# Attention and expert routing on one core: values with the routing, sort in steps, outputs held back, transposes in pairs

## Chip, core and metric

The kernel runs on one core of a Trainium2 chip. The metric is the device time of one execution in microseconds. The kernel before was run three times: 777.58 us in the median, 776.79 to 778.72.

## What is computed

The reference takes x of 4 batches of 1024 tokens of 256 channels, all in float32, and returns `x + attention(xn) + ffn(xn)` with `xn = layernorm(x)`.

```python
xn = layernorm(x)
# attention, 16 heads of 16 channels
q, k, v = heads(xn @ w_q.T), heads(xn @ w_k.T), heads(xn @ w_v.T)
sq = elu(q) + 1
coarse = (sq @ M) / clip(sq @ z)                 # M, z: the four memories summed
fine = sum(softmax(mean over tokens of n_f) * (sq @ memory_m) / clip(n_f))
p = sigmoid(relu(coarse @ eg_w1.T + eg_b1) @ eg_w2.T + eg_b2)
memory = p * fine + (1 - p) * coarse
local = causal_linear_attention(q, k, v, chunk=128)
attention = (g * memory + (1 - g) * local) @ w_o.T    # g = sigmoid(memory_gate)
# ffn: 8 experts of 176, two for each token, and a shared one of 352
cw = normalized top-2 of softmax(xn @ gate_weight.T)
ffn = sum_e cw[e] * swiglu_e(xn) + swiglu_shared(xn)
```

## The kernel before

The 4096 tokens are 8 blocks of 512 (`NBLK`, `TB`), each of 4 tiles of 128 (`NT`); there are 32 tiles (`NTT`). The instructions of each engine run in the order in which the program issues them, and that order is written by hand: a unit is a function with a weight, `mix` merges several streams of units by their share of the total weight, `split` cuts one stream into equal parts, and `run` issues a list. There is no planner beside it.

- **Routing** (`statistics`, `normalize`, `transpose_x`, `logits`). x is loaded on SP's queue, six blocks ahead (`AHEAD`); the weights come on ACT's queue. Each block is normalized in place, written to `xns` in DRAM (later gathered by row), transposed into `xnT`, and multiplied with the gate weights. The reciprocal square root is taken on POOL for two blocks at a time. The first queries are among these units.
- **Sort** (`route`, `sort`, `slots`, `shift_logits`, `weights`, `owners`). DVE finds the two experts of each token and gives each pair a slot; the slots of an expert fill whole tiles, 71 at most (`NST`). `invert` then builds one-hot matrices, three tiles at a time, POOL scales them (`held`, L510), and `add_slots` multiplies them into one PSUM bank (`found`) that lists which token and weight each slot has. These units are mixed with keys and values of block 0, the shared expert of block 0 and the first two attention rounds.
- **Attention rounds.** Round n does, for tile n: `scores` into four PSUM banks (`quad`), `mask` on DVE, `keys_back` (a transpose of the keys), `memory` into the same banks, `weigh` and `fine` on DVE and POOL, `local`, `back` and `update` of the running state. For tile n-1 it does the gate: `turned` transposes coarse, `gate_hidden` multiplies it with `w1` (L830) and ACT takes the relu, `gate_out` multiplies with `w2` (the `pz` matmul, L840). For tile n-2 `turned` transposes o and `output` multiplies the shared expert's hidden layer and o (L895, L899) into `po`.
- **Beside them**, in four parts for each block: `project` for keys and queries, `values` (L578), `shared_gate` and `shared_up`.
- **Experts**, spread over rounds 2 to 29 (`first_round`, `last_round`). For each of 71 slot tiles: `fetch` gathers 128 rows of `xns` on POOL's queue and loads the expert's weights on SP's, `expert_in` transposes the rows (`pxg`, L959), `expert_hidden` multiplies with gate and up (`phe`, L968), `expert_turn` transposes the result (`pTe`, L982), `expert_out` multiplies with down (`pye`, L991), and `put` adds the rows into `sums` in DRAM with an indirect DMA on POOL (L1000). `sums` starts as a copy of x.
- **Tail.** Once all puts have landed, `totals` reads `sums` for tiles 0 to 27, adds the kept outputs on POOL and writes the result; tiles 28 to 31 load their part with `residual` and are added where `output` evicts them.

TensorE's results go through a ring of four PSUM banks (`bank`), shared by everything but `quad`.

Of the kernel before, what the change touches and what calls it, by code (L numbers as in the profile page):

```python
# [8 lines left out]
FP = mybir.dt.float32  # L9
# [5 lines left out]
P = 128  # L15
NT = 4
# [6 lines left out]
def linear_attention_moe_kernel(  # L23
# [51 lines left out]
    AHEAD = 6  # L75
# [10 lines left out]
    big = ctx.enter_context(tc.tile_pool(name="big", bufs=AHEAD))  # L86
# [3 lines left out]
    ps_q = ctx.enter_context(tc.tile_pool(name="ps_q", bufs=1, space=bass.MemoryType.PSUM))  # L90
# [6 lines left out]

    quad = ps_q.tile([P, NG, 512], FP, tag="quad", name="quad")

# [4 lines left out]
    def load_x(blk):  # L104
        xb = big.tile([P, NT, H], FP, tag="tok", name=f"x_{blk}", bufs=AHEAD)
        nc.sync.dma_start(
            xb, x[blk * TB : (blk + 1) * TB, :].rearrange("(n p) h -> p n h", p=P)
        )
        st["x", blk] = xb

    for blk in range(AHEAD):
        load_x(blk)

    def load_weight(w, name):
        t = const.tile([P, NC, w.shape[1]], FP, tag=name, name=name)
        nc.scalar.dma_start(t, w.rearrange("(k p) c -> p k c", p=P))
        return t

    wvg = load_weight(w_vg, "wvg")
    wq = load_weight(w_q, "wq")  # L120
    wk = load_weight(w_k, "wk")
    raw = const.tile([P, NC, NMN, D1], FP, tag="raw", name="raw")
    nc.scalar.dma_start(
# [3 lines left out]
    nc.scalar.dma_start(gate, memory_gate.to_broadcast([P, NH]))  # L127
    b2 = const.tile([P, 1], FP, tag="b2", name="b2")
    nc.scalar.dma_start(b2, eg_b2.to_broadcast([P, 1]))
    w1 = load_weight(eg_w1, "w1")  # L130
    b1 = const.tile([HID, 1], FP, tag="b1", name="b1")
    nc.scalar.dma_start(b1, eg_b1)
    w2 = const.tile([HID, 1], FP, tag="w2", name="w2")
    nc.scalar.dma_start(w2, eg_w2)
# [5 lines left out]
    nc.scalar.dma_start(  # L140
# [3 lines left out]
    if full < NF:  # L144
        nc.scalar.dma_start(wd[: FS - full * P, full, :], w_down[FR + full * P :, :])
# [12 lines left out]
    neghalf = const.tile([P, 2, NT], FP, tag="neghalf", name="neghalf")  # L158
# [64 lines left out]
    alive = const.tile([P, NMN], FP, tag="alive", name="alive")  # L223
    ungate = const.tile([P, NH], FP, tag="ungate", name="ungate")
# [26 lines left out]
    def memories_by_group():  # L251
# [3 lines left out]
        for m in range(3, NMN):  # L255
            nc.vector.tensor_add(raw[:, :, 0, :], raw[:, :, 0, :], raw[:, :, m, :])
        for c in range(NC):
# [18 lines left out]
    def living():  # L276

        norms = small.tile([P, NC, NMN], FP, tag="norms", name="norms", bufs=1)
        nc.vector.tensor_copy(norms, raw[:, :, :, HD])
# [8 lines left out]
    def statistics(blk):  # L288

        xb = st["x", blk]  # L290
        if blk % 2 == 0:
            st["mv"] = small.tile([P, 2, NT, 2], FP, tag="mv", name=f"mv_{blk}", bufs=3)
            st["rstd"] = small.tile([P, 2, NT], FP, tag="rstd", name=f"rstd_{blk}", bufs=3)
        mv, rstd = st["mv"], st["rstd"]
        for i in range(NT):
            stats = small.tile([P, 6], FP, tag="stats", name=f"stats_{blk}_{i}")
            nc.vector.bn_stats(stats, xb[:, i, :])
            nc.vector.bn_aggr(mv[:, blk % 2, i, :], stats)
        if blk % 2:
            nc.vector.tensor_scalar(rstd, mv[:, :, :, 1], LN_EPS, None, ALU.add)  # L300
            nc.gpsimd.tensor_tensor(rstd, rstd, neghalf, ALU.pow)
        st["norm", blk] = mv[:, blk % 2], rstd[:, blk % 2]

    def normalize(blk):
# [9 lines left out]
        nc.vector.tensor_scalar(  # L314
            xb[:, NT - 1, :], xb[:, NT - 1, :], mv[:, NT - 1, 0:1], rstd[:, NT - 1 : NT],
            ALU.subtract, ALU.mult,
        )
        for i in range(NT - 1):
# [7 lines left out]
        if blk + AHEAD < NBLK:  # L326
            load_x(blk + AHEAD)

# [13 lines left out]
    def logits(blk):  # L342

        xnT = st["xnT", blk]
        pl = bank(f"pl_{blk}").rearrange("p (i e) -> p i e", i=NT)
        for i in range(NT):
            for k in range(NC):
                nc.tensor.matmul(
                    pl[:, i, :], xnT[:, k, i * P : (i + 1) * P], wvg[:, k, H + E - P : H + E],
                    start=(k == 0), stop=(k == NC - 1),  # L350
                )
        nc.scalar.copy(lgs[:, blk * NT : (blk + 1) * NT, :], pl[:, :, P - E :])

    def route(half):
# [12 lines left out]
        def first_largest(v, best, m, name):  # L367

            nc.vector.tensor_tensor(m, v, spread(best), ALU.is_equal)
            nc.vector.tensor_mul(m, m, first[:, None, :].to_broadcast(sh))  # L370
            at = t2(name + "_at")
            nc.vector.tensor_reduce(at, m, AX.X, ALU.max)
            nc.vector.tensor_tensor(m, m, spread(at), ALU.is_equal)

# [3 lines left out]
        first_largest(lg, best, m1, "m1")  # L378
# [4 lines left out]
        first_largest(rest, low, m2, "m2")  # L383
        st["best", half] = best

    def shift_logits():
# [8 lines left out]
        nc.scalar.activation(gatew, gatew, AF.Exp)  # L395

    def weights():
# [4 lines left out]
        nc.vector.reciprocal(tot, tot)  # L402
        nc.vector.tensor_mul(gatew, gatew, tot[:, :, None].to_broadcast(sh))
        two = st["two"]
        both = tmp.tile([P, 2, NTT, E], FP, tag="h", name="chosen", bufs=2 * NF)
        nc.vector.tensor_mul(both, picks, gatew[:, None].to_broadcast([P, 2, NTT, E]))
        nc.vector.tensor_reduce(two, both.rearrange("p r i e -> p (r i) e"), AX.X, ALU.add)
        nc.vector.tensor_add(tot, two[:, :NTT], two[:, NTT:])
# [3 lines left out]
        nc.vector.tensor_mul(t2, t2, tot[:, None, :].to_broadcast([P, 2, NTT]))  # L412

    def sort():
# [5 lines left out]
        nc.vector.tensor_add(both, pick[0], pick[1])  # L420
        pp = bank("pp").rearrange("p (w i e) -> p w i e", w=2, e=E)
# [5 lines left out]
        st["pp"] = pp  # L427

    def slots():
        work, pp = st.pop("work"), st.pop("pp")  # L430

        cnt = work[:, 1].rearrange("p (e i) u -> p e (i u)", e=E)
        nc.vector.tensor_copy(cnt, pp[:, 0].rearrange("p i e -> p e i"))
        upto = work[:, 2].rearrange("p (e i) u -> p e (i u)", e=E)
# [306 lines left out]
    def update(n):  # L741

        if n % (BPB * NT) == last_of_batch:
            return
# [464 lines left out]
```

## Time and profile before

| | |
|---|---|
| median of three runs | 777.58 us |
| the profiled execution: time, span | 782.79 us, 781.1 us |
| TensorE busy, mean granted clock | 700.7 us (90%), 0.956 |
| DVE, POOL, ACT busy | 426.1, 400.3, 273.8 us |
| bytes moved | 81.48 MB, mean 104 GB/s |

The profile is of one execution, with times from the start of its span. In names such as `phe L968` the number is a line of the kernel. A matmul in float32 appears as two records, a transpose as one. A matmul's busy time includes the drain of its pipeline, so records next to each other overlap. In the stage tables the columns are: the stretch, its length, the busy time of TensorE, of its weight loads (PEld), of DVE, ACT and POOL, each with the number of instructions, then the granted TensorE clock, the busy share of the DMA engines and GB/s. In the lists of groups, `busy, mean ns | idle before` is followed by what ended the idle time.

### The profile page before, as it was taken

What the parts mean: (1) busy time and instruction counts of PE and PEld (TensorE: products, weight loads), DVE (VectorE), ACT (ScalarE), POOL (GpSimd) and SP (SyncE); (2) the same over time, 40 slices, a digit from 0 to 9 for tenths busy, and PEclk for the clock granted to TensorE, in tenths of its full rate; (3) what the DMA queues carried; (4) which work ended last, traced back from release to release, by engine and by line L of the source; (5) the groups of instructions that cost most, each with busy time, mean ns of one, the idle gap of its engine ahead of it and who ended that gap; (6) DMA issues with size and microseconds to landing.
All of it is one profiled execution on the core that took longest, in us unless ns stands there. A gap on an engine that the chain in (4) does not pass through costs nothing.

```text
span 781.1 us, 14630 instructions
## 1 busy us (share of the span) xinstructions
PE 700.7 (90%) x5268; PEld 491.0 (63%) x5268; DVE 426.1 (55%) x1084; ACT 273.8 (35%) x707; POOL 400.3 (51%) x441
## 2 busy tenths in 40 slices
PE   1798579499999999999999999999999999999965
PEld 0675356366676666666667667666766667767653
DVE  6536857445446744455536644554457555655553
ACT  2563002123443333433443343433443344334300
POOL 3100366506555656464546555556545646657576
PEclk9899689889999999999999999999999999999976
DMA  9554000234343453344444443443443444454285
GB/s 283 183 178 134 1 0 1 59 107 97 84 117 85 90 118 84 86 106 94 97 111 92 103 104 84 93 113 84 97 104 85 107 101 103 108 123 99 29 261 171
DMA packets 86373, 81.48 MB, mean 104 GB/s; under 512 B 7437, under 2 KB 83901, under 8 KB 86173
## 3 DMA queue, kind: packets, MB, share of 16 engines
q1 hardware_dynamic: 69661, 59.64, 26.5%
q0 software_dynamic: 13632, 18.62, 14.3%
q10 hardware_dynamic: 3008, 2.28, 0.9%
q8 instruction: 42, 0.69, 0.4%
q14 instruction: 30, 0.25, 0.1%
HBM read 62.56 MB, written 22.15 MB: 108 GB/s over the span
## 4 chain that ended last, share of the span: by engine, by line
PE 76%; DVE 7%; DMA 5%; POOL 4%; ACT 3%; issue 3%; SPq 0%; POOLq 0%; DVEq 0%; ACTq 0%
PE phe L968 12%; PE pye L991 8%; PE po L895 5%; PE psu L871 5%; PE pg L856 5%; PE quad L658 4%; PE pn L684 4%; PE po L899 3%; PE pv L578 3%; PE pq L550 3%; PE pk L550 3%; PE quad L770 3%; PE pxg L959 2%; PE pTe L982 2%; PE ph L830 2%
## 5 line engine op out<-in xcount | busy, mean ns | idle before, releaser
L1000 POOL DMA_INDIRECT sums<-y,islot x71 | 112.7, 1588 | 81.0 <-DMA sums<-y,islot 29.9
L792 POOL TENSOR_TENSOR cg<-coarse,gates 128x256 f32<-128x256 f32 x32 | 23.7, 742 | 165.1 <-DVE coarse L785 164.9
L968 PE MATMUL phe<-wgu,xgT 128*128 128x352 f32 x284 | 100.9, 478 | 1.1 <-ACT hTe L984 0.9
L665 DVE TENSOR_TENSOR sT<-quad,causal 128x512 f32<-128x512 f32 x128 | 80.2, 682 | 14.3 <-PE pk L736 6.5
L933 POOL DMA_INDIRECT xg<-xns,islot x71 | 71.3, 1005 | 15.9 <-issue 8.8
L991 PE MATMUL pye<-wdn,hTe 88*128 88x256 f32 x284 | 76.6, 392 | 1.8 <-ACT oT L822 1.0
L968 PEld LDWEIGHTS phe<-wgu,xgT 128*128 128x128 f32 x284 | 49.9, 191 | 25.3 <-issue 5.3
L810 POOL TENSOR_TENSOR fm<-fm 128x512 f32<-128x512 f32 x32 | 43.6, 1363 | 36.5 <-DVE prob L843 23.1
L974 DVE SCALAR_TENSOR_TENSOR the<-the,phe 128x176 f32<-128x176 f32 x71 | 23.8, 335 | 69.6 <-ACT the L973 66.8
L991 PEld LDWEIGHTS pye<-wdn,hTe 88*128 88x128 f32 x284 | 49.5, 189 | 15.1 <-issue 5.5
L995 ACT ACTIVATE y<-pye,wslot 128x256 f32<-128x256 f32 x71 | 33.6, 473 | 58.6 <-PE pye L991 55.7
L895 PE MATMUL po<-wd,h 128*128 128x256 f32 (+1 forms) x192 | 49.2, 394 | 0.0
L973 ACT ACTIVATE the<-phe 128x176 f32<-128x176 f32 x71 | 22.5, 318 | 74.5 <-PE phe L968 72.5
L871 PE MATMUL psu<-xnT,wu 128*128 128x512 f32 (+1 forms) x96 | 47.6, 620 | 0.0
L856 PE MATMUL pg<-xnT,wg 128*128 128x512 f32 (+1 forms) x96 | 47.0, 613 | 0.7 <-ACT nT L691 0.7
L799 DVE TENSOR_TENSOR fm<-quad,rw 128x512 f32<-128x512 f32 x64 | 42.0, 682 | 0.0
L863 DVE SCALAR_TENSOR_TENSOR th<-th,pg 128x512 f32<-128x512 f32 (+1 forms) x24 | 16.4, 684 | 43.8 <-ACT th L862 39.6
L876 DVE SCALAR_TENSOR_TENSOR h<-th,psu 128x512 f32<-128x512 f32 (+1 forms) x24 | 16.5, 686 | 42.9 <-PE psu L871 42.2
L961 ACT COPY xgT<-pxg 128x256 f32<-128x256 f32 x71 | 26.5, 373 | 37.1 <-PE pxg L959 18.3
L895 PEld LDWEIGHTS po<-wd,h 128*128 128x128 f32 (+1 forms) x192 | 36.1, 200 | 4.3
L558 DVE SCALAR_TENSOR_TENSOR sqT<-pq,eq 128x512 f32<-128x512 f32 x16 | 11.1, 692 | 50.8 <-ACT eq L556 50.7
L563 DVE SCALAR_TENSOR_TENSOR skT<-pk,ek 128x512 f32<-128x512 f32 x16 | 11.1, 691 | 49.8 <-ACT ek L556 47.1
(195 smaller groups left out, 1510.2 us busy)
## 6 DMA issues: line engine op xcount, KB each, us to landing
wgu<-in_w_gate_dram SPq DMA_DIRECT2D x71, 176.0 KB
wgu<-in_w_up_dram SPq DMA_DIRECT2D x71, 176.0 KB
wdn<-in_w_down_dram SPq DMA_DIRECT2D x71, 176.0 KB
x<-in_x_dram SPq DMA_DIRECT2D x8, 512.0 KB
xns<-x SPq DMA_DIRECT2D x8, 512.0 KB
sums<-in_x_dram SPq DMA_DIRECT2D x8, 512.0 KB
part<-sums SPq DMA_DIRECT2D x14, 256.0 KB
out_dram<-acc SPq DMA_DIRECT2D x14, 256.0 KB
```

Of the source, the lines that this page charges most:

```text
L550: nc.tensor.matmul(pq, w[:, k, c * P : (c + 1) * P], xnT[:, k, :], start=(k == 0), stop=(k == NC - 1),)
L665: nc.vector.tensor_mul(sT, quad[:, g, :].rearrange("p (c t) -> p c t", t=P), causal[:, None, :].to_broadcast([P, NC * 2, P]),)
L799: nc.vector.tensor_mul(fm[:, c].rearrange("p g m (r k) -> p g (m r) k", k=HD), quad[:, :, c * KM + KX + KN : (c + 1) * KM].rearrange("p g ...
L810: nc.gpsimd.tensor_add(fm[:, :, 0:2, :], fm[:, :, 0:2, :], fm[:, :, 2:4, :])
L856: nc.tensor.matmul(pg[:n, :], wg[:, k, f * P : f * P + n], xnT[:, k, :], start=(k == 0), stop=(k == NC - 1),)
L871: nc.tensor.matmul(pu[:n, :], wu[:, k, f * P : f * P + n], xnT[:, k, :], start=(k == 0), stop=(k == NC - 1),)
L895: nc.tensor.matmul(po[:, :H], st["h", blk, f][:k, tok], wd[:k, f, :], start=(f == 0), stop=False)
L933: nc.gpsimd.indirect_dma_start(out=xg, out_offset=None, in_=xns, in_offset=bass.IndirectOffsetOnAxis(ap=islot[:, j : j + 1], axis=0),)
L968: nc.tensor.matmul(ph[:, : 2 * F], xgT[:, k, :], wgu[:, k].rearrange("p g f -> p (g f)"), start=(k == 0), stop=(k == NC - 1),)
L991: nc.tensor.matmul(py[:, :H], hT[:, f, :], wdn[:, f, :], start=(f == 0), stop=(f == 1))
L995: nc.scalar.activation(y, py[:, :H], AF.Copy, scale=wslot[:, j : j + 1])
L1000: nc.gpsimd.indirect_dma_start(out=sums, out_offset=bass.IndirectOffsetOnAxis(ap=islot[:, j : j + 1], axis=0), in_=st.pop(("y", j)), in_of ...
```

## The change

The kernel after does the same arithmetic with these edits:

- **Loads.** All eight blocks of x are loaded at the start on SP's queue. Only the weights of values, queries and keys stay on ACT's queue; the others follow x on SP's.
- **Values with the routing.** `values` works on two tiles, with the gate weights as eight more columns, and gives the logits as well; the separate `logits` go. The values of all blocks are computed in the routing and are written into the tile that held x. The routing's order is a written list. Queries move out of it.
- **Statistics.** Block 0 takes its reciprocal square root alone, the others in pairs 1-2, 3-4, 5-6, and 7 alone. DVE normalizes two of four tiles, not one.
- **Sort in steps.** `route`, `sort`, `slots` (now in `sort`), `weights` and `owners` are generators, cut into 32 steps that are mixed with the queries of blocks 0 to 2, keys of 0 and 1 and the shared expert of block 0. `projected` and `shared_hidden` hold the last DVE step of a projection and are issued one unit later.
- **Lists in rounds 0 to 3.** `invert`, `hold` and `add_slots` stand three batches apart; ACT scales the tokens, POOL the weights. The experts run over rounds 4 to 29, after a pause of weight 2000.
- **Gate.** coarse becomes the stationary operand and `w1` the moving one; bias, relu, the product with `w2` and its sum are on DVE, and `pz` goes.
- **Transposes.** `turned` takes o of tile n-2 and coarse of n-1 in one bank with one copy; `keys_back` takes two tiles every second round; `expert_turn` takes the hidden layer of slot tile j and the gathered rows of j+2 in one bank with one copy.
- **Outputs held back.** The outputs of tiles 24 to 31 are computed after round 29, mixed with rounds 30 and 31, and add their part of `sums` on DVE; `totals` covers tiles 0 to 23. Results are written on ACT's queue.
- Some buffers shrink (`nT`, `loc`, `coarse`, `cg`, `o`, `sk` to one, `xg` from four to three).

```diff
-    for blk in range(AHEAD):
+    for blk in range(NBLK):
         load_x(blk)
...
-    def logits(blk):
+    def values(blk, pair):
+        xnT, wide = st["xnT", blk], st["wide", blk]
+        if pair == 0:
+            st["va", blk] = wide[:, :, : NH * D1].rearrange("p i (h k) -> p i h k", k=D1)
+        va = st["va", blk]
+        pv = ps_v.tile([P, 2, 512], FP, tag="v", name=f"pv_{blk}_{pair}")
+        for j in range(2):
+            i = 2 * pair + j
             for k in range(NC):
                 nc.tensor.matmul(
-                    pl[:, i, :], xnT[:, k, i * P : (i + 1) * P], wvg[:, k, H + E - P : H + E],
+                    pv[:, j, : H + E], xnT[:, k, i * P : (i + 1) * P], wvg[:, k, :],
                     start=(k == 0), stop=(k == NC - 1),
                 )
...
+        nc.scalar.copy(
+            va[:, tiles, :, :HD], pv[:, :, :H].rearrange("p i (h k) -> p i h k", k=HD)
+        )
+        nc.scalar.copy(lgs[:, first : first + 2, :], pv[:, :, H : H + E])
...
+    def hold(lo):
...
+        for k in range(n):
+            nc.scalar.activation(
+                held[:, k, 0], tiles[:, k], AF.Copy, scale=token[:, lo + k : lo + k + 1]
+            )
+        nc.gpsimd.tensor_mul(
+            held[:, :, 1], tiles, st["two"][:, lo : lo + n, None].to_broadcast([P, n, NST])
+        )
...
+    def turned(n):
+        srcs = [(s, m) for s, m in (("o", n), ("coarse", n + 1)) if 0 <= m < NTT]
+        pt = bank(f"pt2_{n}").rearrange("p (s c t) -> p s c t", s=2, t=P)
...
     def gate_hidden(n):
...
-                ph[:HID, :P], w1[:, c, :], cT[:, c, :], start=(c == 0), stop=(c == NC - 1)
+                ph[:, :HID], cT[:, c, :], w1[:, c, :], start=(c == 0), stop=(c == NC - 1)
-        nc.scalar.activation(h1, ph[:HID, :P], AF.Relu, bias=b1)
+        nc.vector.tensor_add(h1, ph[:, :HID], b1)
+        nc.vector.scalar_tensor_tensor(h1, h1, 0.0, w2, ALU.max, ALU.mult, accum_out=z)
...
     def gate_out(n):
...
-        nc.tensor.matmul(pz[:, :1], st.pop(("h1", n)), w2, start=True, stop=True)
-        nc.scalar.activation(prob, pz[:, :1], AF.Tanh, bias=b2, scale=0.5)
+        nc.scalar.activation(prob, st.pop(("z", n)), AF.Tanh, bias=b2, scale=0.5)
...
+    def expert_turn(j):
+        fetch_rows(j + 4)
+        fetch_weights(j + 3)
+        pt = bank(f"pte_{j}").rearrange("p (f t) -> p f t", t=P)
+        lo, hi = (0 if j >= 0 else 2), (4 if j + 2 < NST else 2)
+        if j >= 0:
+            for f in range(2):
+                nc.tensor.transpose(pt[:, f, :], hidden[j % 2][:, f * FH : f * FH + P], ident)
+        if j + 2 < NST:
+            xg = st.pop(("xg", j + 2))
+            for c in range(NC):
+                nc.tensor.transpose(pt[:, 2 + c, :], xg[:, c * P : (c + 1) * P], ident)
+        dst = exp.tile([P, 4, P], FP, tag="turned", name=f"turned_{j}")
+        nc.scalar.copy(dst[:, lo:hi], pt[:, lo:hi])
...
-    first_round, last_round = 2, 30
+    first_round, last_round = 4, 30
...
+    ahead = "S0 S1 masks N0 T0 S2 S3 N1 N2 V0 T1 T2 S4 memories V1 S5 N3 N4 V2 T3 T4 S6 gates V3 S7"
+    ahead += " N5 N6 V4 living T5 T6 N7 V5 route V6 T7 V7"
...
+    first_pairs = queries(0) + queries(1) + keys(0) + shared(0) + keys(1) + queries(2)
+    start = [u for u in late(first_pairs) if u]
...
+    run(mix(steps(sorting(), 32, 1000), start))
...
+    for k, lo in enumerate(batches):
+        lists += [(400, invert, lo)]
+        lists += [(100, hold, batches[k - 1])] if k else []
+        lists += [(768, add_slots, batches[k - 2])] if k > 1 else []
...
+    units = [(10, residual, n) for n in range(held_from, held_from + 3)]
+    outs = {n: [(1280, output, n, True)] for n in range(held_from, NTT)}
...
+    units[2:2] = [(1800, lambda: None)]
+    tail = mix([u for n in range(last_round, NTT) for u in rounds[n]], units)
```

In the written list S is `statistics`, N `normalize`, T `transpose_x` and V `values` of a block; `held_from` is 24.

## The prediction

> **What bounds the kernel now.** I read the page first, then a table of busy time by stage, the start times of TensorE's instructions in the middle, and the chain that ended last. From the page: TensorE's share, the granted clock in 40 slices, and the dearest group on POOL.
>
> ```profile
> PE 700.7 (90%) x5268; PEld 491.0 (63%) x5268; DVE 426.1 (55%) x1084; ACT 273.8 (35%) x707; POOL 400.3 (51%) x441
> ...
> PEclk9899689889999999999999999999999999999976
> ...
> L1000 POOL DMA_INDIRECT sums<-y,islot x71 | 112.7, 1588 | 81.0 <-DMA sums<-y,islot 29.9
> ```
>
> Five of the first nine slices show 6 or 8 tenths of the clock, the last two 7 and 6: TensorE starves in the first quarter and at the end. The stages, cut at 70 (routing), 146 (sort, lists, rounds 0 and 1), 156 (first gathered rows land), 733 (rounds 2 to 29 with the experts) and 742 (last put lands):
>
> ```profile
> 0.00:70.00 70.00, 45.78 (x238) 35.34 (x239) 35.38 (x151) 30.87 (x66) 10.99 (x35) 0.93 0.68 217
> 70.00:90.00 20.00, 12.88 (x73) 6.52 (x71) 17.26 (x50) 2.98 (x7) 0.52 (x1) 0.81 0.00 0
> 90.00:120.00 30.00, 22.86 (x147) 17.45 (x148) 16.28 (x31) 1.90 (x4) 20.08 (x28) 0.77 0.00 1
> 120.00:146.00 26.00, 23.38 (x170) 17.66 (x168) 21.70 (x46) 6.94 (x16) 18.11 (x29) 1.00 0.00 1
> 146.00:156.00 10.00, 0.58 (x4) 0.29 (x2) 2.83 (x7) 1.38 (x3) 4.62 (x5) 0.66 0.37 105
> 156.00:733.00 577.00, 565.08 (x4390) 389.74 (x4388) 312.92 (x758) 223.13 (x596) 314.04 (x315) 0.99 0.43 98
> 733.00:742.00 9.00, 7.21 (x103) 5.61 (x102) 3.05 (x6) 2.96 (x9) 5.06 (x5) 1.00 0.28 32
> 742.00:781.00 39.00, 22.91 (x152) 18.36 (x152) 16.69 (x37) 3.60 (x10) 26.86 (x26) 0.69 0.67 216
> ```
>
> The columns after the length are TensorE, its weight loads, DVE, ACT, POOL, clock, DMA share and GB/s. The middle is TensorE at 98%; from 70 to 156 TensorE has 59.7 us of work in 86, behind DVE and POOL; the tail moves 8.4 MB of sums and outputs in 39 us.
>
> Busy time counts a group's pipeline tail, so I price TensorE work from start to start:
>
> ```profile
> 410.14 0.38 PE L840 MATMUL pz<-w,h 64*128 64x1 f32 x2
> 410.45 0.44 PE L959 MATMUL pxg<-ident,xg 128*128 128x128 f32 x2
> 410.73 0.60 PE L700 MATMUL pb<-ident,nT 128*128 128x128 f32 x4
> ```
>
> pz is shown as 0.38 but costs 0.31, and the two transposes 0.28. The chain of waits over 156 to 733, summed by line, gives such prices for all lines. An attention round costs 8.4 us (scores 1.15, memory 0.79, local 1.02, back 1.03, update 0.47, output 2.16, gate_hidden 0.58, pz 0.31, transposes of o, coarse and keys 0.27, 0.34, 0.28). An expert step costs 2.82 (phe 1.30, pye 0.96, pxg 0.29, pTe 0.27). A block's keys and queries cost 3.5 each, shared projections 10.8, values 3.6. Check: 28 rounds, 71 steps and 6.5 blocks without the last queries give 235 + 200 + 136 = 571 of the measured 577.
>
> **The change, stage by stage.** The sum is made for the profiled execution: span 781.1, time 782.79, so 1.7 around it; the median of the runs is 777.58, a factor of 0.9933.
>
> *Front, to the end of the last values: 67 us.* Block 0 gets its own rstd, so transposes start near 12 instead of 16. All logits matmuls go (eight groups of 16 at 1.79 us, 14.3), 8 columns are added to each value matmul, and all values come in (8 x 3.7). Values write into x's own tile, so ACT's first copy waits until the write of xns from that tile has landed, and behind it on ACT are the copies of blocks 1 and 2, for which TensorE waits. On SP's queue lie 4.2 MB of x, 1.4 of weights now moved there and the 0.5 written; with 0.8 on ACT's queue that is 7 MB. The first 20 us moved 286 GB/s, so it lands near 25 to 28, and TensorE, with transposes of blocks 0 to 2 and values 0 done (4 + 3.7, cold at first), idles from about 22 to 29. What such a gap does to the clock is shown by the same stretch of before:
>
> ```profile
> 25.00:30.00 5.00, 2.46 (x19) 1.79 (x17) 2.46 (x10) 1.78 (x4) 0.00 (x0) 0.97 0.43 138
> 30.00:35.00 5.00, 3.78 (x20) 3.59 (x20) 2.69 (x13) 1.15 (x4) 0.25 (x1) 0.68 0.87 301
> 35.00:40.00 5.00, 4.09 (x19) 3.62 (x20) 2.34 (x19) 4.74 (x11) 1.70 (x3) 0.66 0.36 126
> ```
>
> Two half-idle slices cost about 3 us at a clock of 0.67. The Trainium skill (TensorE: Matmul & The Clock Gate, Part 1) speaks against a change that opens such a gap: after an idle window of about 3.4 us the clock halves, until a window of that length is busy. By it the cost is an estimated 1.7 us; I keep the row's 3.
>
> From 29 on there are 7 x 3.7 of values and 5 x 1.33 of transposes, 33 us, and 5 for the cold clock and the last block's copies: 67. ACT (3.7 per block: two normalizations of 0.53, four copies) and DVE (3.3) stay under TensorE's 5.2. Ends 60 (the write lands early) and 76 (every xns takes 5.9 us to land, as the second did).
>
> *Sort: 35 us.* 16 projection units of 1.76 to 1.79, 28.4, and 1.5 of small matmuls; beside them DVE has about 14 of sort steps, 6 of projected and 8 of gating, 4 of batch weights: 32. The two are nearly equal and DVE serves in order, so 35; ends 31 and 42.
>
> *Rounds 0 to 3 with the lists: 72 us.* TensorE: four rounds without pz, two of them without output, shared(1), 128 found matmuls of 0.13: 53. DVE: 8.7 per round less 2 (33), shared gating 8.2, invert 22 times. An invert costs 0.92 (L499 0.37, L503 0.55) where POOL rests and 1.6 (0.71, 0.89) beside L510; half of L510 moves to ACT, so I take 1.15: 25. DVE sums to 66 and now sets the pace; with waits for scores and memory 72, ends 63 and 84. The first rows' landing (4.25) lies under the pause ahead of the experts.
>
> *Rounds 4 to 29: 502 us.* Per round pz goes (0.31), and o and coarse stand side by side, and where pairs already did, they started 0.21 to 0.22 apart instead of 0.27 and 0.34: 0.18. So 7.9 x 26 = 205. gate_hidden moves 64 columns instead of 128 but loads 128 instead of 64; I book no gain, since even pz with one moving column takes 0.15 each. Outputs 24 to 27 leave (8.6). Experts 71 x 2.77 = 197, by the same reason. Gathers move behind put and out on POOL and stay two turns ahead of use; weights stay three ahead on SP. Projections of blocks 2 to 7: 6 x 17.8 less 3.5, 103, and 1.5 for batch weights. Sum 498, and 1% as in before. The added DVE pair in gate_hidden (some 0.45) replaces 0.36 on ACT and pz's wait; DVE, at 11.2 per round now (312.92 over 28), hides it. ACT loses a fixed part of one copy per expert step (0.373 + 0.363 against 0.59 for 512 columns) and is no bound. Buffers cut to one are read and rewritten a round apart. Ends 486 (turns gain 0.15 more each) and 525 (a round of 20.2).
>
> *Tail: 44 us against 48 from 733.* The last put still lands some 8 after the last experts. Eight outputs (17) stand where TensorE was idle 18 us, and loads no longer queue behind outputs on SP. But ACT, which issues the outputs now, waits for POOL's totals, and behind it are nT and the turned copies of rounds 30 and 31. The chain shows that the DMA sets this pace:
>
> ```profile
> 738.21 3.71 DMA sums<-y,islot
> ...
> 743.41 4.40 DMA part<-sums
> ```
>
> The same 8.4 MB at 237 GB/s (740 to 760) takes 35, plus the end of the chain. Ends 38 and 52.
>
> Sum 67 + 35 + 72 + 502 + 44 = 720, with 1.7 it is 721.7, times 0.9933: 717.
>
> **Rivals.** *The middle is held by something else than TensorE's issue.* Its weight loads are busy 389.7 of 577 and some 40 us of the chain there are ACT, DVE and issue. Then a round keeps its 20.6, 26 x 20.6 = 536, and the time is 751. Against it: the priced instructions fill 571 of 577. The Trainium skill (Perfetto Trace Analysis, Identifying the Most-Contended Engine) says matmul busy time is a poor measure of headroom and the share of weight loads a better one; by it (68% here) TensorE would not be the limit, which is this case. Chance 0.17.
>
> *Front, lists and tail at their good ends* (60, 31, 63, 502, 38): 691 to 700; DVE would have to run the lists without waits. 0.12.
>
> *Slower: POOL's puts.* A put waits on POOL for the one before it to land, and gathers and attention's sums stand behind it. POOL's work per round becomes 5.3 for attention, 2.73 x 1.59 puts and 2.73 x 1.0 gathers, 12.4. If each put took the cycle of the last two (3.71 to land and 1.57 before, 5.3), a round would need 5.3 + 2.7 + 14.4 = 22.4 us: 582 for the middle, 797 in all. It turns slower from 21.7 per round. For it: steps come every 7.0 us instead of 8.1, and each merged turn now holds the hidden layer until the gathered rows are there. Against: waits for earlier puts total 29.9 us over 71, and 7.0 is above 5.3. 0.09, and 0.03 for a balance within 0.3%, about what a measurement of this kernel tells from no change.
>
> **Numbers.** The forecast, 717 (700 to 738), has 0.59. The ends of the terms, taken together as independent, give some 25 either way; the first rival reaches 751. So 694 to 750. Faster 0.88, same 0.03, slower 0.09.
>
> **What would show it.** Values end near 67 and the first scores start near 102. TensorE is near 98% busy from 174 to 676, a round taking 19.3. In rounds 0 to 3 DVE is over 85% busy. If TensorE is near 98% and rounds still take 20.6, my prices are wrong; if TensorE is idle there behind pte or phe, POOL's puts are the place to look. A front past 76 means that the copies of values wait for xns.

## The result, and the profile after

The changed kernel takes 731.43 us in the median of four runs (731.18 to 731.93); the kernel before, run beside it, takes 778.15. The ratio is 0.9397, with a 95% interval of 0.9373 to 0.9422: 6% faster. The forecast was 717, its range 694 to 750. The profiled execution took 731.18 us with a span of 729.5. From here on "the changed kernel" is this one, and experiments are compared by their ratios to the kernel before, since chips differ by a few tenths of a per cent.

The page of the changed kernel, with the rows that answer to those of before:

```profile
PE 653.1 (90%) x5084; PEld 465.3 (64%) x5084; DVE 455.9 (62%) x1193; ACT 266.8 (37%) x614; POOL 386.0 (53%) x436
...
PEclk9799989999999999999999999999999999999598
...
L1058 POOL DMA_INDIRECT sums<-y,islot x71 | 113.4, 1597 | 70.6 <-DMA sums<-y,islot 15.1
```

TensorE has 47.6 us less work and keeps its 90%. Of the first nine slices of the clock two are below 9 (a 7 and an 8) instead of five; near the end there is a 5. Waits of a put for the put before it fell from 29.9 to 15.1 us, although the experts now run in two rounds fewer: the slower rival, POOL's puts, found nothing to stand on.

The stages, cut where the last values end, where the scores of rounds 0, 4 and 30 start, and at the end of the last put:

```profile
0.00:60.30 60.30, 40.98 (x197) 34.76 (x198) 29.49 (x133) 27.27 (x64) 13.41 (x68) 0.92 0.69 222
60.30:89.50 29.20, 29.00 (x73) 12.92 (x71) 23.82 (x66) 14.00 (x25) 0.00 (x0) 1.00 0.19 64
89.50:165.10 75.60, 58.88 (x573) 45.56 (x573) 63.10 (x142) 27.99 (x89) 35.43 (x45) 0.93 0.06 15
165.10:672.00 506.90, 489.54 (x3957) 344.50 (x3956) 315.68 (x795) 191.89 (x422) 306.82 (x293) 0.99 0.49 111
672.00:682.80 10.80, 3.36 (x57) 2.53 (x56) 5.70 (x15) 0.53 (x2) 6.20 (x7) 0.75 0.27 33
682.80:729.50 46.70, 31.39 (x234) 24.99 (x234) 18.11 (x45) 5.15 (x14) 24.09 (x24) 0.83 0.57 180
```

Against the forecast's terms: front 60.3 (67), sort 29.2 (35), rounds 0 to 3 75.6 (72), rounds 4 to 29 506.9 (502), tail 57.5 (44). The differences are -6.7, -5.8, +3.6, +4.9 and +13.5, in all +9.5. Against before, cut at the same scores: round 4 starts at 165.1 instead of 201.3, rounds 4 to 29 take 506.9 instead of 531.7, and from round 30 to the end it is 57.5 instead of 48.1; that is -36.2 - 24.8 + 9.4 = -51.6, the whole difference of the spans. So the tail gives back 9.4 of 61.0 us, and that is where the forecast is furthest off.

The forecast of 717 is 14.4 us below the measured 731.43. The terms account for 9.5 of that. The other 5 come from the factor 0.9933: the profiled execution of before was slower than its kernel's median, that of the changed kernel was not (731.18 against 731.43). And 9.5 is a small remainder of large misses: -12.5 in the front and the sort against +13.5 in the tail. That they nearly cancel is luck.

What TensorE waited for, by line (total, times, longest), of the changed kernel:

```profile
PE ph L879 <- ACT oc L868: 14.4, 2, 12.0
PE pt L344 <- ACT x L331: 11.2, 1, 11.2
PE found L568 <- POOL held L560: 9.6, 6, 3.0
PE quad L806 <- DVE sT L698: 9.1, 5, 2.4
PE pv L362 <- ACT xnT L347: 8.2, 2, 7.8
```

The second is the start. Of the others, three name places to test: the tail behind ACT (first), the lists behind POOL's `held` (third), the front behind ACT's copies of the transposed xn (last).

### The profile page after: what moved, and what is told of

It is laid out like the page before. It is cut to its first block, busy times and chain, and to the rows that moved or that the text cites. A ratio compares the mean times of both kernels' runs of the same rounds, so it can differ in the third digit from the quotient of the medians.

```text
span 729.5 us, 14268 instructions
## 1 busy us (share of the span) xinstructions
PE 653.1 (90%) x5084; PEld 465.3 (64%) x5084; DVE 455.9 (62%) x1193; ACT 266.8 (37%) x614; POOL 386.0 (53%) x436
## 5 line engine op out<-in xcount | busy, mean ns | idle before, releaser
L1058 POOL DMA_INDIRECT sums<-y,islot x71 | 113.4, 1597 | 70.6 <-DMA sums<-y,islot 15.1
L1042 DVE SCALAR_TENSOR_TENSOR hidden<-hidden,phe 128x176 f32<-128x176 f32 x71 | 23.8, 335 | 122.4 <-ACT hidden L1041 122.4
L1036 PE MATMUL phe<-wgu,turned 128*128 128x352 f32 x276 | 96.9, 474 | 2.5 <-ACT turned L1029 2.1
L1049 PE MATMUL pye<-wdn,turned 88*128 88x256 f32 x284 | 75.5, 388 | 4.2 <-PE pu L786 3.0
L1036 PEld LDWEIGHTS phe<-wgu,turned 128*128 128x128 f32 x276 | 48.5, 191 | 26.2 <-issue 6.4
L1049 PEld LDWEIGHTS pye<-wdn,turned 88*128 88x128 f32 x284 | 50.1, 189 | 20.1 <-issue 8.5
L846 POOL TENSOR_TENSOR fm<-fm 128x512 f32<-128x512 f32 x32 | 41.7, 1304 | 26.2 <-DVE prob L892 13.1
L1041 ACT ACTIVATE hidden<-phe 128x176 f32<-128x176 f32 x71 | 22.6, 318 | 86.7 <-PE phe L1036 79.7
L1029 ACT COPY turned<-pte 128x512 f32<-128x512 f32 (+1 forms) x71 | 41.2, 580 | 35.6 <-PE pte L1027 34.6
L362 PE MATMUL pv<-wvg,xnT 128*128 128x264 f32 x128 | 33.1, 420 | 8.2 <-ACT xnT L347 8.2
L806 PE MATMUL quad<-mem,sqT 32*128 32x170 f32 x512 | 27.6, 328 | 9.1 <-DVE sT L698 9.1
L894 DVE SCALAR_TENSOR_TENSOR o<-diff,prob,loc 128x256 f32<-128x256 f32 x32 | 33.1, 1035 | 3.4
```

The costliest lines, as they stand in the source:

```text
L846: nc.gpsimd.tensor_add(fm[:, :, 0:2, :], fm[:, :, 0:2, :], fm[:, :, 2:4, :])
L1029: nc.scalar.copy(dst[:, lo:hi], pt[:, lo:hi])
L1036: nc.tensor.matmul(ph[:, : 2 * F], xgT[:, k, :], wgu[:, k].rearrange("p g f -> p (g f)"), start=(k == 0), stop=(k == NC - 1),)
L1049: nc.tensor.matmul(py[:, :H], hT[:FH, f, :], wdn[:, f, :], start=(f == 0), stop=(f == 1))
L1058: nc.gpsimd.indirect_dma_start(out=sums, out_offset=bass.IndirectOffsetOnAxis(ap=islot[:, j : j + 1], axis=0), in_=st.pop(("y", j)), in_of ...
```

## The experiments

### The tail: who issues the outputs

In the tail of the changed kernel, ACT's waits and its timeline read so:

```profile
ACT oT L865 <- POOL acc L980: 22.5, 2, 15.8
ACT oT L865 <- DMA out_dram<-acc: 6.7, 1, 6.7
```
```profile
687.86 0.46 ACTq L981 DMA_DIRECT2D out_dram<-acc  x1
688.36 0.37 ACT L865 COPY oT<-pt 128x256 f32<-128x256 f32 x1 [15.83 <-POOL acc L980]
688.62 0.38 ACT L868 COPY oc<-pt 128x256 f32<-128x256 f32 x1
```

The turned o and coarse lay in their bank since 674; the copy ran at 688.36, behind the write of a total that POOL had to finish first. ACT's write sits in ACT's order of instructions and holds everything behind it. Theory: this block is what makes the tail 13 us too long. Rival: the DMA engines set the tail, whoever issues.

**e1, outputs issued by SP.**

```diff
-        nc.scalar.dma_start(out[n * P : (n + 1) * P, :], acc)
+        nc.sync.dma_start(out[n * P : (n + 1) * P, :], acc)
...
-        nc.scalar.dma_start(
+        nc.sync.dma_start(
             out[n * P : (n + 2) * P, :]
```

> Only change to the kernel after: the output writes of the tail go back from ACT's queue to SP's. Theory (ACT is blocked): in the tail ACT waits 15.8 us for POOL's first totals before a write, TensorE idles 12 behind it, and later 6.7 and 6.7 on ACT again. Without that the idle 12 us shrink to what the landing of the first res needs, some 5 to 7, and the tail (672 to 729.5, 57.5 us) falls to 46 to 50: about 721 to 724 against 731.4. Rival (the DMA rate and the last put set the tail): the 8.4 MB still have to move after the last put, and the time stays within 2 us of 731.4.

Measured: 0.9251 [0.9217, 0.9285], 1.6% below the changed kernel. From the scores of round 30 to the end it takes 44.2 us instead of 57.5, more of a gain than expected (46 to 50). ACT's waits in the tail name POOL no more, and the stage moves more bytes per second; below them the stage's row:

```profile
ACT nT L724 <- PE pn L717: 13.4, 3, 7.3
ACT oT L865 <- PE pt L860: 12.2, 4, 4.9
```
```profile
675.00:719.20 44.20, 33.95 (x291) 27.20 (x290) 23.70 (x57) 5.70 (x16) 29.04 (x29) 0.91 0.63 197
```

The theory holds, and 44.2 is the forecast's 44. The stage now moves 197 GB/s; over the 57.5 us of the changed kernel it was 153, so the DMA engines were not the limit there.

**e2, four outputs held back instead of eight.**

```diff
-    held_from = NTT - 2 * NT
+    held_from = NTT - NT
```

> Only change to the kernel after: outputs are held back from tile 28 on instead of 24, so outputs 24 to 27 run in rounds 26 to 29 and totals covers tiles 0 to 27. Theory (TensorE's issue sets the middle, the tail has room): the middle grows by 4 x 2.16 = 8.6 us and the tail shrinks by less than that, 2 to 5, since TensorE idles there anyway: 735 to 738. Rival (the held outputs cost in the tail what they save before it): within 2 us of 731.4.

Measured: 0.9495 [0.9469, 0.9521], 1% slower than the changed kernel, some 8 us where 4 to 7 were expected, so holding back eight pays. But not where it was priced: the rounds 26 to 29, which get outputs 24 to 27 back, take 67.3 us instead of 65.9, only 1.4 more, not 8.6. Even that is within the scatter: in the runs that hold back eight and have the same code there (the changed kernel, e1, e5, e6, e7, e9) these rounds took 65.4 to 67.5. The busy times of these rounds tell why, first in the changed kernel, then with four:

```profile
606.10:672.00 65.90, 59.05 (x549) 42.64 (x548) 44.33 (x104) 23.42 (x56) 42.99 (x41) 0.97 0.48 105
```
```profile
608.20:675.50 67.30, 65.95 (x589) 49.04 (x588) 42.37 (x107) 24.49 (x56) 41.25 (x39) 1.00 0.45 102
```

TensorE's work grew by 6.9 us and the stretch by 1.4: without those outputs TensorE is idle there for 6.9 us. Taking work from the engine that bounds the average round paid little in these four, which are short of other work. The tail, with ACT still blocked, took 60.3 us though it had half the outputs; `nT`, behind totals on ACT, held TensorE for 10.8 us at once.

### The parts that should make the middle shorter

**e3, the gate as before** (64 x 128 with Relu on ACT, pz back).

```diff
-                ph[:, :HID], cT[:, c, :], w1[:, c, :], start=(c == 0), stop=(c == NC - 1)
+                ph[:HID, :P], w1[:, c, :], cT[:, c, :], start=(c == 0), stop=(c == NC - 1)
...
-        nc.vector.tensor_add(h1, ph[:, :HID], b1)
-        nc.vector.scalar_tensor_tensor(h1, h1, 0.0, w2, ALU.max, ALU.mult, accum_out=z)
+        nc.scalar.activation(h1, ph[:HID, :P], AF.Relu, bias=b1)
...
+        nc.tensor.matmul(pz[:, :1], st.pop(("h1", n)), w2, start=True, stop=True)
```

> Only change to the kernel after: the gate is computed as before, w1 stationary with 128 moving columns, bias and relu on ACT, and the matmul with w2 (pz) back on TensorE. Theory (the middle is priced by TensorE's starts): 0.31 us per round for pz and some 0.1 for ph (0.48 to 0.58 start to start), so 32 x 0.4 = 10 to 13 us: 741 to 744. Rival (something else holds the rounds): within 2 us of 731.4, or faster, since DVE has two instructions less per round.

Measured: 0.9471 [0.9439, 0.9502], 0.8% slower, some 6 us where 10 to 13 were expected. Rounds 4 to 29 take 520.9 instead of 510.1 in e1 on the same chip (which differs there only in who issues the results), +10.8: TensorE's issue, as expected (0.4 us for pz and the other form of the gate's matmul, times 26, is 10.4). The rows of rounds 4 to 29, first e1, then e3:

```profile
164.90:675.00 510.10, 489.44 (x3957) 344.51 (x3956) 315.32 (x798) 191.46 (x422) 308.22 (x295) 0.99 0.47 111
```
```profile
161.70:682.60 520.90, 506.63 (x4013) 350.22 (x4012) 291.11 (x721) 201.62 (x449) 309.26 (x295) 0.99 0.46 108
```

Rounds 0 to 3 became 3.2 shorter (72.6 against 75.8 in e1). That fits DVE, which has the most work there and no longer does the gate: 58.31 us busy instead of 63.02. So the gate's move pays in the middle and costs in the lists.

The Trainium skill (Perfetto Trace Analysis, Identifying the Most-Contended Engine) would judge TensorE's headroom by the share of its weight loads. That share was 67.5% in e1's middle and 67% in e3's, a third free by that rule; yet one small matmul more per round (two records) and the other form of the gate's matmul made the stage longer by 10.8 us. In this case the measurement decides against reading a third of headroom from that share. The prediction went further and took 68% to mean that TensorE would not be the limit. That does not follow: in e1's middle DVE is at 62% and POOL at 60%, so TensorE leads by that share too.

**e4, pairs side by side but each in its own bank with its own copy.** The part for the experts is shown; o and coarse are parted in the same way.

```diff
-        pt = bank(f"pte_{j}").rearrange("p (f t) -> p f t", t=P)
...
-        nc.scalar.copy(dst[:, lo:hi], pt[:, lo:hi])
+            pt = bank(f"pTe_{j}").rearrange("p (f t) -> p f t", t=P)
...
+            nc.scalar.copy(dst[:, 0:2], pt[:, 0:2])
...
+            px = bank(f"pxg_{j}").rearrange("p (f t) -> p f t", t=P)
...
+            nc.scalar.copy(dst[:, 2:4], px[:, 0:2])
```

> Only change to the kernel after: the transposes stay side by side on TensorE, but those of o and of coarse, and those of the hidden layer and of the gathered rows, each have a bank and a copy of their own. Theory (sharing the bank and the copy is worth little, the place beside each other is): TensorE's starts stay, ACT gets 71 x 0.15 + 30 x 0.15 = 15 us more work at 37% busy, and the time stays within 3 us of 731.4. Rival (the ring of four banks or ACT's latency sets the pace): each expert step waits for a bank, 0.1 us or more for 71 steps and 30 rounds, so 10 us or more: 741 and above.

Measured: 0.9626 [0.9599, 0.9654], 2.4% slower than the changed kernel; rounds 4 to 29 take 524.2, 14 more than e1. I had expected less than 3 us, so my theory falls: standing side by side does not keep the gain, sharing the bank and the copy does. The run does not tell the bank from the copy.

**e10, transposes apart as in the kernel before.**

```diff
-    def turned(n):
+    def turned(key, m):
...
+        pt = bank(f"pt{key}_{m}").rearrange("p (c t) -> p c t", t=P)
...
+    def expert_in(j):
...
-            u += [(256, turned, n - 2)]
+        u += [(128, turned, "o", n - 2)]
...
-                units += [(704, expert_hidden, j)]
+                units += [(704, expert_hidden, j), (256, expert_in, j + 2)]
```

> To the kernel after, the transposes are taken apart again as before the change: o ahead of the second mask and coarse ahead of the fourth, the gathered rows right behind the hidden layer's matmul and the hidden layer itself behind the output's matmul, each with a bank and a copy of its own. Theory of the prediction (each group pays its own start, 0.27 to 0.34 us for a pair instead of 0.21): 30 x 0.18 + 71 x 0.05 to 0.1, so 9 to 13 us more, 740 to 744. Rival (only groups that stand side by side in two banks exhaust the ring of four, as in the kernel with two banks; apart they find a free bank): within 4 us of 731.4. Second rival (every bank more costs, wherever it stands): 745 and above.

Measured: 0.9739 [0.971, 0.9768], 3.6% slower than the changed kernel, some 27 us, where the prices of the prediction gave 8 and I had expected 9 to 13. Of the 3.6%, 2.4% are bank and copy (e4); the places apart add the rest. Its rounds 4 to 29 take 531.8, as long as in the kernel before; the changed kernel takes 506.9 there, and e1, e5, e6 and e7, with the same code in these rounds, 510 to 512. Of the parts of the change that these runs take out again this is the largest, and I had booked it as one of the smallest.

Where these 20 to 25 us of the middle sit, TensorE's starts show. In the changed kernel four pairs follow each other at 0.21 to 0.27 us and the next matmul starts at once:

```profile
308.04 0.44 PE L1023 MATMUL pte<-ident,hidden 128*128 128x128 f32 x2
308.31 0.38 PE L1027 MATMUL pte<-ident,xg 128*128 128x128 f32 x2
308.53 0.38 PE L860 MATMUL pt<-ident,o 128*128 128x128 f32 x2
308.75 0.38 PE L860 MATMUL pt<-ident,coarse 128*128 128x128 f32 x2
308.96 1.35 PE L1036 MATMUL phe<-wgu,turned 128*128 128x352 f32 x4
```

In e10 a typical bad place looks like this:

```profile
207.18 0.40 PE L1015 MATMUL pxg<-ident,xg 128*128 128x128 f32 x2
...
207.62 0.37 ACT L1017 COPY xgT<-pxg 128x256 f32<-128x256 f32 x1 [1.29 <-PE pxg L1015]
...
208.05 1.13 PE L1045 MATMUL pye<-wdn,hTe 88*128 88x256 f32 x4 [0.46 <-ACT xgT L1017]
```

The pair takes 0.87 us to the next start, and the matmul behind it, which does not read xgT, starts only when that copy is through. I summed such stretches over rounds 4 to 25, each pair from its start to the start of the next group, and counted as stalls those of 0.6 us or more:

| kernel | pairs | followed by a stall | their time, us | all transposes of o, coarse, hidden, rows, us |
|---|---|---|---|---|
| before | 155 | 2 | 1.9 | 42.7 |
| changed | 167 | 4 | 3.2 | 42.4 |
| e4, own banks | 167 | 32 | 26.2 | 61.7 |
| e10, apart | 167 | 23 | 24.1 | 63.2 |

A pair without a stall costs about the same everywhere (median 0.22 to 0.27). What sharing takes away is the stalls. But the kernel before had its transposes apart and stalled twice: its price of 0.14 per transpose was right there and wrong in the new surroundings. Something else in the change makes apart dear, and sharing covers it.

How the stalls end is in the traces. In 30 of the 32 of e4 and 19 of the 23 of e10 the next group starts 0.05 us after the end of an ACT instruction on whose semaphore it waits. Nearly all are copies out of a bank, often of another bank than the pair's own; a DVE instruction ends two stalls in e4 and one in e10.

The last two runs asked what makes apart dear: theory 1, the gate's bank, which now waits for DVE; theory 2, the order of the expert's transposes.

**e11, apart with the old gate** (e10 with e3's edit), **and e12, apart with the old order of the expert's transposes.**

```diff
-                units += [(704, expert_hidden, j), (256, expert_in, j + 2)]
+                units += [(704, expert_hidden, j), (128, expert_in, j + 1)]
...
-            units += [(256, expert_turn, j)] if j < NST else []
+            units += [(128, expert_turn, j)] if j < NST else []
```

The edit shown is e12's, against e10; e11's is that of e3.

> The version with all transposes apart, and the hidden layer of the gate computed as in the kernel before too (64x128, Relu by ACT, pz on TensorE). There the transposes apart cost 0.20 us each (from start to start) and a round 20.5, but in the kernel before they cost only 0.14. Theory 1, the gate's bank is now held until DVE has added and multiplied, and transposes apart wait for that bank in the ring of four: the transposes fall back to some 0.14 to 0.15, 18 to 20 us over rounds 4 to 29, against the 10.8 that pz and its bank cost; on the scale where the kernel before is 780.1 and the version apart 759.8 the time is 750 to 753. Theory 2, the order does it (the gathered rows are turned two steps ahead of their use, behind phe): the transposes stay at 0.20 and the old gate costs its 10.8, 768 to 771.

> The version with all transposes apart, with the order of the expert's transposes as in the kernel before: gathered rows turned one step ahead, each transpose with weight 128 in the mix, gathers two ahead. Theory 1, the gate's bank on DVE: nothing changes, 758 to 762 on the scale where the version apart is 759.8. Theory 2, the order: transposes of gathered rows and of the hidden layer fall from 0.20 to 0.14 each, 71 x 4 x 0.06 = 17 us, 741 to 745. If neither run moves them, the dearer transposes come from something else that both runs share, such as DVE's fuller queue.

Measured: e11 0.968 [0.9641, 0.9719], e12 0.9778 [0.9711, 0.9845]; e10 was 0.9739. The order does nothing that the measurement can tell (27 stalls of 23.4 us): theory 2 falls. The old gate brings the stalls to 15 of 14.4 us and the transposes to 58.8, so theory 1 explains 4 to 10 of the 20 us at most; rounds 4 to 29 take 535.3, 3.5 more than e10, where the same edit had cost 10.8 in e3. And the mechanism of theory 1 is not what the ends of the stalls show, which wait for ACT. e11's time, 755 on the scale of its expectation, comes near the 750 to 753 of theory 1 all the same, but by another stage: what it gains over e10 in all comes from its rounds 0 to 3 (73.8 us against 78.2). The larger part stays open. Differences from before that I did not try: 22.5 us of value matmuls stood between the short groups in rounds 4 to 25, and now they are in the front; six buffers shrank to one; and 71 slot tiles are spread over 26 rounds instead of 28.

### The lists

**e5, the held weights scaled by ACT, not POOL.**

```diff
-        nc.gpsimd.tensor_mul(
-            held[:, :, 1], tiles, st["two"][:, lo : lo + n, None].to_broadcast([P, n, NST])
-        )
+            nc.scalar.activation(
+                held[:, k, 1], tiles[:, k], AF.Copy, scale=st["two"][:, lo + k : lo + k + 1]
+            )
```

> Only change to the kernel after: in hold, ACT scales the token weights as well, so POOL has no part in the lists. Theory (DVE sets rounds 0 to 3, slowed by POOL's part beside it): TensorE's 9.6 us of waits for held go, an invert falls from 1.28 us to 1.0 and less, and rounds 0 to 3 fall from 75.6 to 66 to 70; ACT gets 64 more copies of 0.34, 22 us, in 76 at 37% busy, which fits: 722 to 726 against 731.4. Rival (ACT then is the bound of these rounds, 28 + 22 us and in order with the copies of nT and the transposes): within 2 us, or up to 3 slower.

Measured: 0.9348 [0.9325, 0.9371], 0.5% faster, some 4 us where 5 to 9 were expected. TensorE waits 1.1 us for `held` instead of 9.6, and rounds 0 to 3 take 69.5 instead of 75.6. The two halves of an invert, first in the changed kernel, then in e5:

```profile
L544 DVE TENSOR_TENSOR ones<-count,lohi 128x384 f32<-128x384 f32 (+1 forms) x22 | 16.6, 754 | 0.0
L540 DVE TENSOR_TENSOR ones<-count,lohi 128x213 f32<-128x213 f32 (+1 forms) x22 | 12.0, 545 | 3.2 <-issue 3.2
```
```profile
L544 DVE TENSOR_TENSOR ones<-count,lohi 128x384 f32<-128x384 f32 (+1 forms) x22 | 15.0, 683 | 0.0
L540 DVE TENSOR_TENSOR ones<-count,lohi 128x213 f32<-128x213 f32 (+1 forms) x22 | 10.5, 479 | 2.5 <-PE found L568 2.5
```

An invert falls from 1.30 to 1.16 us, not to the expected 1.0 or less. DVE is slower while POOL works beside it, as the 0.92 and 1.6 of before had said, and in e5 POOL still works on attention. The single instructions show it, here for the 21 batches of full size: with no POOL instruction beside them the halves take 0.55 and 0.37 us in the changed kernel and in e5 alike, with ACT busy beside them or idle; with POOL busy beside them for at least 90% of their time they take 1.05 and 0.72 in the changed kernel. In e5, 15 and 13 stand without POOL, in the changed kernel 4 and 8. Of the 6.1 us gained in the stage some 4 reached the end.

### The front

**e6, the 1.4 MB of weights loaded after the first writes of xns.**

```diff
-    w1 = load_weight(eg_w1, "w1")
...
+    def late_loads():
...
-    ahead = "S0 S1 masks N0 T0 S2 S3 N1 N2 V0 T1 T2 S4 memories V1 S5 N3 N4 V2 T3 T4 S6 gates V3 S7"
+    ahead = "S0 S1 masks N0 T0 S2 S3 N1 N2 V0 T1 T2 S4 memories V1 S5 N3 N4 loads V2 T3 T4 S6 gates V3 S7"
```

> Only change to the kernel after: w1, wo, wg, wu, wd, b1 and w2 (1.4 MB) are loaded on SP's queue after the writes of xns of blocks 0 to 4, not ahead of them. Theory (the copies of the first values wait for the write of xns, which stands behind these loads): the write lands 4 to 5 us earlier, TensorE's gap from 19.5 to 27.5 shrinks to 3 or 4, and the end of the values moves from 60.3 to 55 to 57: 727 to 729. Rival (the gap has another cause: ACT's order or the normalization of block 1): the end of the values stays at 60.

Measured: 0.927 [0.9254, 0.9285], 1.4% faster; the values end at 51.2 instead of 60.3, more than expected (55 to 57). In the changed kernel ACT's first copy of the values waits until the write of xns from its tile has landed, and TensorE's front reads as below it:

```profile
25.71 0.59 ACT L367 COPY x<-pv 128x512 f32<-128x512 f32 x1 [7.97 <-DMA xns<-x]
```

```profile
17.77 1.91 PE L344 MATMUL pt<-ident,x 128*128 128x128 f32 x16
27.48 9.77 PE L362 MATMUL pv<-wvg,xnT 128*128 128x264 f32 x32 [7.81 <-ACT xnT L347]
37.09 1.91 PE L344 MATMUL pt<-ident,x 128*128 128x128 f32 x16
```

In e6 the same place:

```profile
18.19 1.91 PE L347 MATMUL pt<-ident,x 128*128 128x128 f32 x16
20.58 7.39 PE L365 MATMUL pv<-wvg,xnT 128*128 128x264 f32 x32 [0.48 <-ACT xnT L350]
27.80 1.91 PE L347 MATMUL pt<-ident,x 128*128 128x128 f32 x16
```

In e6 ACT has no such wait. The gap of 7.81 us is gone, and the 32 matmuls behind it take 7.22 us from start to start instead of 9.61. The clock of the changed kernel there:

```profile
25.00:30.00 5.00, 2.52 (x6) 2.00 (x7) 2.29 (x9) 3.19 (x8) 2.44 (x13) 0.50 0.40 140
30.00:35.00 5.00, 5.00 (x19) 4.09 (x18) 1.48 (x8) 1.94 (x6) 1.64 (x1) 0.77 0.00 0
35.00:40.00 5.00, 5.00 (x33) 4.46 (x32) 0.00 (x0) 4.61 (x12) 0.30 (x4) 1.00 0.60 208
```

0.50, then 0.77, then 1.00, where e6 has 1.00 in all three: the clock costs 9.61 - 7.22 = 2.4 us. The Trainium skill (TensorE: Matmul & The Clock Gate, Part 1) says half the clock after an idle window of some 3.4 us, until one such window is busy. The 0.50 agrees, and the measured 2.4 lies between the 1.7 that the prediction estimated by it and the 3 that it kept.

### Together

**e7** joins e1, e5 and e6; **e8** is e7 with four outputs held back; **e9** is e7 with the totals added by DVE:

```diff
-        nc.gpsimd.tensor_add(acc, acc, st.pop(("part", n)))
+        nc.vector.tensor_add(acc, acc, st.pop(("part", n)))
```

> The three edits together: output writes on SP's queue, hold wholly on ACT, the 1.4 MB of weights after the writes of xns 0 to 4. Theory (three separate stalls in three stages): the gains add up, 11 for the writes and what the two single runs show, together 18 to 25: 706 to 713 against 731.4. Rival (one stage's gain comes back as a wait in the next): less than two thirds of the sum.

> The three edits together (writes on SP, hold on ACT, weights later), and outputs held back from tile 28 on only. Theory (rounds 26 to 29 are not held by TensorE: with and without the four outputs they took 67.3 and 65.9 us; and a tail without ACT's block has no room to spare): the middle grows by 1 to 2 and the tail shrinks by up to 4, so holding eight is worth nothing or less once ACT is free: 704 to 708 on the scale on which the three together take 707. Rival (holding back is worth what was priced, 8.6 in the middle against a few in the tail): 712 and above.

> As the three edits together, and the sums of totals are made by DVE instead of POOL. Theory (with the writes on SP the tail's chain is POOL's 12 totals of 1.25 us between the attention's sums): POOL is freed of 15 us, DVE takes 12 x 0.7 = 8 and has the room (18 of 33 us busy), and the tail falls by 3 to 6 us. Rival (DVE is in order: an add that waits for its part to land holds the masks of round 31 and the evictions behind it, or the DMA rate of 250 GB/s is the limit): within 2 us of the kernel without this edit, or slower.

Measured: e7 707.25 us, 0.9048 [0.903, 0.9066]; e8 0.9103 [0.9071, 0.9135]; e9 0.9121 [0.9108, 0.9135]. The three repairs add up: 1.55% + 0.5% + 1.35% is 3.4%, and e7 is 3.7% below the changed kernel. It is the best version. With ACT free, holding eight is still better than four by 0.6%, where I had expected nothing or less: 1.4 us in rounds 26 to 29, as in e2 and no more than their scatter, and 3.1 in the tail (44.9 against 48.0), which I had expected to shrink. Totals on DVE are worse, as the rival said: they take 54.5 us from round 30 on instead of 44.9, with

```profile
PE quad L809 <- DVE sT L701: 14.0, 2, 13.7
```

This is e1's lesson once more, on another engine: the scores' mask queues behind a total that waits for its rows.

## Why the prediction was right, and where it was not

The time lies in the range and on the forecast's side because the mechanism of the middle was right: TensorE's issue sets the round, pz and the gate's matmul are worth what their starts show (e3), and a round takes 19.5 us against the forecast's 19.3. That the total comes within 2% of the forecast is partly luck, as the terms above show. The rival "held by something else" would have left 536 us there; it is 506.9.

The step that failed is the tail's. The prediction named the block (ACT issues the outputs, waits for POOL's totals, and nT and the turned copies stand behind it) and then took 44 us and an upper end of 52 from the DMA's bytes, without a price for it. It costs 13.3 us (57.5 against e1's 44.2), and 57.5 is past the end. A wait that is named needs its row: the total's rows landing and POOL's sum ahead of the issue.

Terms that were mis-sized, by size:

- *Pairs of transposes*, 0.18 us per round and 0.05 per step, about 8 us in all: taking them apart again in the changed kernel costs 27 (e10). The total came out near all the same, since the sum started from the prices of before, where apart was cheap. Against these the saving is smaller than booked: from start to start o and coarse together take 0.44 us a round instead of 0.56, and an expert step's two pairs 0.53 instead of 0.55, some 5 us in all (means of rounds 4 to 25). Within the changed kernel the saving is in stalls that before did not have; a price per instruction could not show it.
- *Outputs 24 to 27 leaving the middle*, 8.6: 1.4 (e2). The rounds that lose them become short of other work.
- *Front*, 67: 60.3. The gap came where it was forecast (19.5 to 27.5, forecast 22 to 29), and its clock cost 2.4 instead of 3. From there to the end it took 32.8 us, not 38. The matmuls were taken too dear: the transposes of a block take 0.87 us at full clock (16 in 1.74, for two blocks, at 37.09), not 1.33, and a block's values 3.6 (e6), not 3.7. That makes 29.6, and the clock's 2.4 are the rest but for 0.8.
- *Sort*, 35: 29.2. DVE was taken at 32 and had 23.82, so it never held TensorE, which is busy 29.00 of 29.20. My estimate of DVE's work there was 8 us too high.
- *Rounds 0 to 3*, 72: 75.6. An invert was taken at 1.15 and takes 1.30, which is 22 x 0.15 = 3.3 more; but DVE's work in all was 63.1, less than the 66 of the sum, so that does not explain the miss. Too small were the waits: 12.5 us of the stage are without DVE work, where 6 were booked, and TensorE waits 9.6 for `held`; with that gone (e5) the stage takes 69.5. DVE is busy 83%, a little under the 85% that the text asked for. In e3 and e5 it has 4.7 us less to do, and the stage is 3.2 and 6.1 shorter, which fits that its work there counts.

The good-ends rival got the front and the sort about right and the rest wrong. The front past 76 did not come: the first copies did wait for xns (e6), but once, not in every block.

## What to carry to other kernels

ACT did nothing else for 15.8 us while a write that it had to issue waited for its data. Put writes that wait for late data on a queue whose engine has no other work, and price the block if you can't. Where short transposes go through a small ring of banks, count banks and copies as well as instructions: sharing one bank and one copy was worth 14 us of rounds 4 to 29 (e4), the gate's matmuls 10.8 (e3). A saving read from the average round must be checked against the round that it is taken from, since there another engine may already be next.

## What the runs showed of the hardware that I had not expected

- A pair of transposes in banks of their own costs 0.22 to 0.27 us in the median like any other, but one in five to seven of them (32 and 23 of 167) held the next group of matmuls for 0.6 us or more in e4 and e10, against 4 of 167 with a shared bank; the list of waits shows only some of that as idle time. Nearly all of these waits (30 and 19) end with an ACT instruction, mostly a copy out of a bank. Why these copies hold TensorE here and not in the kernel before is not settled.
- The two DVE instructions of an invert take 0.92 us without POOL beside them and 1.77 with POOL busy for at least 90% of their time (changed kernel). ACT busy beside them does not slow them (0.37 and 0.55 in e5 too). Moving POOL's share to ACT took the mean from 1.30 to 1.16 and 3.0 us off DVE's work for the 22 inverts.
- 7.8 us without matmuls cost 2.4 us more behind the gap through the clock: this late load was paid for a third more than it was late.
